# Second cross-attention of a Perceiver block: two key periods per loop step instead of one

## The chip, the cores and the metric

The kernel runs on one core of a Trainium2 chip. Five engines work side by side, each taking its instructions in the order in which they are written: TensorE (PE, matrix multiply, with its weight load PEld shown apart), VectorE (DVE), ScalarE (ACT), GpSimd (POOL) and SyncE (SP, which here only starts DMA transfers). They wait for one another by semaphores. The metric is the device time of one execution in microseconds. The kernel before took 1573.84 us, the median of three runs (1573.14 to 1574.27).

## The reference, cut to what matters

The program computes two layers of a Perceiver: each has a cross-attention to a long context, a self-attention and a mixture-of-experts network. All data is 32-bit float. The change touches only the cross-attention of the second layer. The state `x` has 128 rows (queries) of 256; the context has 12544 rows of 192.

```python
HEADS = 16
DIM_HEAD = 64
q = x @ Wq
k = context @ Wk
v = context @ Wv
...
sim = jnp.einsum('bhid,bhjd->bhij', q, k) * SCALE
attn = jax.nn.softmax(sim, axis=-1)
out = jnp.einsum('bhij,bhjd->bhid', attn, v)
...
return out @ Wo + bo
```

Here `x` is the layer-normalised state. So keys and values of 12544 rows x 1024 columns must be projected, and 16 heads of 128 x 12544 scores go through a softmax.

## The kernel before, in words

**Tiling.** Two heads make a pass (`PASSES` = 8): their 2 x 64 columns fill 128 partitions. The context is cut into 13 blocks (`NS`) of up to 1024 rows, the last with 256. A period `t` is one pass and one block, 104 in all (`NP`). What a period computes is spread over 15 turns of the loop, since the softmax needs the maximum over a whole pass before it can take exponentials. Scores of period `t` are made and kept in SBUF (a ring of 28 slots of 128 x 1024). `LAG` = 14 turns later their exponentials meet the values.

**Four kinds of matmul work in a turn.** A 32-bit matmul is issued as two matmuls in the trace.

- `scores` (L977): keys times queries, 64 rows deep. The two heads sit in rows 0 to 63 and 64 to 127 of the array and run side by side: row tiles.
- `project_keys` (L210, L213) and `project_values` (L228, L235): 192 rows deep, done as a whole part of 128 rows (`whole`, L213 and L235) and a rest of 64 rows (`tiled`, L210 and L228), where the two halves of the block run side by side as row tiles. `tiled` opens the accumulation in its PSUM bank, `whole` closes it.
- `attend` (L1069): exponentials times values, 64 columns wide. The two heads run side by side as column tiles.

**Order.** The order is written by hand (`manual_schedule`): each engine does its work as the code lists it. In one turn PE does: `attend` of period `t`-14 (column tiles), `scores` of `t`, the tiled parts of the keys of `t`+1 and of the values of `t`-12 (row tiles), then the whole parts of keys and values.

**The other engines.** ACT copies each score tile to its slot (L994), takes the exponentials (L1057) and evicts the values (L962) and half of the keys (L948). DVE keeps the running maximum (L1001), evicts the other half of the keys (L950), sums the exponentials over keys (`added`, L1096) and adds the output of `attend` to its accumulator (`attended`, L1113). POOL subtracts the maximum from the kept scores (`shifted`, L1051: the negated maximum, spread over all partitions, is added) and adds up the partial sums (L1101). SP loads the context blocks, two buffers each.

**At the end of a pass** `fold` reduces the maximum (L1024), `pass_maximum` transposes it on PE (L246) and reduces it on DVE (L1029), `pass_spread` transposes it back (L251) and ACT stores it (L1042). In the next turn but one `pass_end` sums the denominators on PE (L1124), and DVE divides (L1129, L1130). The first two periods of a pass are shifted and exponentiated at once after the maximum is known, so as to be ready for `attend`.

**PSUM.** Of eight banks, four belong to two score tiles (`ps_s`, two banks each), and four (`ps_w`) are handed round among the output of `attend`, the two halves of the keys, the two halves of the values and the small transposes. A bank can be written again once its readers are done.

Of the kernel before, what the change touches and what calls it, by code (L numbers as in the profile page):

```python
# [8 lines left out]
F32 = mybir.dt.float32  # L9
AF = mybir.ActivationFunctionType  # L10
ALU = mybir.AluOpType
# [22 lines left out]
def perceiver(ctx: ExitStack, tc: tile.TileContext, a: dict, out: bass.AP):  # L34
# [18 lines left out]
    def ps_w(name):  # L53
        return banks["pool"].tile([P, KB], F32, tag="w", name=name, bufs=banks["w"])
# [143 lines left out]
            )  # L198
        return lo, hi, h

    def project_keys(name, wk, cx, j, bank=None):

        lo, hi, h = cx
        ps = [(bank or ps_w)(f"{name}_{r}") for r in range(2)]
        js = slice(j * P, (j + 1) * P)

        def tiled():
            for r in range(2):
                rs = slice(64 * r, 64 * r + 64)
                nc.tensor.matmul(ps[r][:, :h], wk[1][rs, js], hi[rs, :h], start=True, stop=False)  # L210

        def whole(r):
            nc.tensor.matmul(ps[r][:, :h], wk[0][:, js], lo[:, r * h : (r + 1) * h], start=False, stop=True)  # L213

        return ps, tiled, whole

    def project_values(name, wv, cx, j, bank=None):

        lo, hi, h = cx
        ps = [(bank or ps_w)(f"{name}_{r}") for r in range(2)]  # L220
        js = slice(j * P, (j + 1) * P)

        def tiled():
            for kc in range(h // P):
                ks = slice(kc * P, (kc + 1) * P)
                for r in range(2):
                    rs = slice(64 * r, 64 * r + 64)
                    nc.tensor.matmul(  # L228
                        ps[r][:, ks], hi[rs, ks], wv[1][rs, js], start=(kc == 0), stop=False,
                        skip_group_check=True,  # L230
                    )

        def whole(r):
            for kc in range(h // P):
                nc.tensor.matmul(  # L235
                    ps[r][:, kc * P : (kc + 1) * P], lo[:, r * h + kc * P : r * h + (kc + 1) * P],
                    wv[0][:, js], start=False, stop=True, skip_group_check=True,
                )

        return ps, tiled, whole  # L240
# [61 lines left out]
    with tc.tile_pool(name="l0w", bufs=1) as lw:  # L302
# [8 lines left out]
        with tc.tile_pool(name="l0x", bufs=1) as work, ExitStack() as ps0:  # L311
# [195 lines left out]
            def shift(engine, t, k, banks, by):  # L507
                if banks.stop > banks.start:
                    v = ps[t][k].rearrange("p (a c n) -> p a c n", a=2, c=2)[:, banks]
                    n = banks.stop - banks.start  # L510
                    engine.tensor_tensor(v, v, by[:, banks].unsqueeze(2).to_broadcast([P, n, 2, 256]), ALU.add)  # L511
# [383 lines left out]
    with tc.tile_pool(name="l1x", bufs=1) as work:  # L895
# [31 lines left out]
        def tiles_of(s):  # L927

            n = min(SB, SK - s * SB) // P
            return [(0, 4), (4, 4)] if n == 8 else [(0, n)]  # L930
# [4 lines left out]
            place = slot if t >= NP and (t - NP) % 3 == 2 else None  # L935
            ctxs[t] = load_context(work, f"x1_ctx{t}", (t + 1) % NS, 2, place=place)

        def keys(t):
            j, s = periods[t]
            kTs[t] = work.tile([P, SB], F32, tag="kT", name=f"x1_kT{t}", bufs=2)  # L940
            cx = ctxs[t - 1]
            h = cx[2]
            pk, tiled, whole = project_keys(f"x1_k{t}", ywk, cx, j)

            def out(r):
                dst = kTs[t][:, r * h : (r + 1) * h]
                if r:
                    nc.scalar.copy(dst, pk[r][:, :h])  # L948
                else:
                    nc.vector.tensor_copy(dst, pk[r][:, :h])  # L950

            return tiled, whole, out

        def values(t):
            j, s = periods[t]
            vs[t] = work.tile([P, 8, P], F32, tag="v", name=f"x1_v{t}", bufs=3)
            cx = ctxs[t + LAG - 2]
            n = cx[2] // P
            pv, tiled, whole = project_values(f"x1_v{t}", ywv, cx, j)

            def out(r):
                nc.scalar.copy(  # L962
                    vs[t][:, r * n : (r + 1) * n, :].rearrange("p k d -> p (k d)"), pv[r][:, : n * P]
                )

            return tiled, whole, out
# [16 lines left out]
        def scores_kept(p, n):  # L983
            return p.rearrange("p (a n) -> p a n", a=2)[:, :, : n * P]

        def keep(t, sts, between=None):

            j, s = periods[t]
            ps[t] = [slot(f"x1_p{t}_{i}") for i in range(len(sts))]
            if s == 0:  # L990
                mx[j] = work.tile([P, 2, KB], F32, tag="mx", name=f"x1_mx{j}")

            def copy(i):
                nc.scalar.copy(scores_kept(ps[t][i], sts[i].shape[2] // P), sts[i])  # L994

            def maximum(i):
                n = sts[i].shape[2] // P
                if s == 0 and i == 0:
                    return
                old = scores_kept(ps[t][0], 4) if s == 0 else mx[j][:, :, : n * P]  # L1000
                nc.vector.tensor_tensor(mx[j][:, :, : n * P], sts[i], old, ALU.max)  # L1001

            if j == 0:

                for i in range(len(sts)):
                    copy(i)
                for i in range(len(sts)):
                    if s or i:
                        n = sts[i].shape[2] // P
                        m = mx[j][:, :, : n * P]  # L1010
                        old = scores_kept(ps[t][0], 4) if s == 0 else m
                        nc.vector.tensor_tensor(m, scores_kept(ps[t][i], n), old, ALU.max)
                return
            copy(0)
            if between is not None:
                between()
            if len(sts) == 2:
                maximum(1)
                copy(1)
            maximum(0)  # L1020
# [10 lines left out]
        def pass_spread(j):  # L1031
            spreads[j] = work.tile([P, 2, P], F32, tag="spread", name=f"x1_spread{j}", bufs=2)
            if j == PASSES - 1:

                final["sums"] = ps_s("x1_sums")
                final["both"] = ps_s("x1_both")
            pb = ps_w(f"x1_mb{j}")
            if j == PASSES - 1:
                final["spread"] = pb
            for u in range(2):  # L1040
                spread_column(pb[:, u * P : (u + 1) * P], negm[j][:, u : u + 1])
            nc.scalar.copy(spreads[j].rearrange("p u q -> p (u q)"), pb[:, : 2 * P])  # L1042

        def shifted(t):
            j, s = periods[t]
            for i, (p, (c0, n)) in enumerate(zip(ps[t], tiles_of(s))):
                v = p.rearrange("p (a c q) -> p a c q", a=2, q=P)[:, :, :n, :]
                engine, by = nc.gpsimd, spreads[j]
                if j == PASSES - 1 and (i == 0 or s == 0):
                    engine, by = nc.vector, final["spread"][:, : 2 * P].rearrange("p (u q) -> p u q", q=P)  # L1050
                engine.tensor_tensor(v, v, by.unsqueeze(2).to_broadcast([P, 2, n, P]), ALU.add)  # L1051

        def exponents(t):
            j, s = periods[t]
            for p, (c0, n) in zip(ps[t], tiles_of(s)):
                v = scores_kept(p, n)
                nc.scalar.activation(v, v, AF.Exp)  # L1057

        def attend(t):
            j, s = periods[t]  # L1060
            whole = j == PASSES - 1
            o = final["both"][:, 0] if whole else ps_w(f"x1_o{t}")
            total = sum(n for c0, n in tiles_of(s))
            for p, (c0, n) in zip(ps[t], tiles_of(s)):
                for c in range(n):
                    for u in range(2):
                        us = slice(64 * u, 64 * u + 64)
                        n0 = KB * u + c * P
                        nc.tensor.matmul(  # L1069
                            o[us, 0:P], vs[t][:, c0 + c, us], p[:, n0 : n0 + P],  # L1070
                            start=(c0 + c == 0 and (s == 0 or not whole)),
                            stop=(c0 + c == total - 1 and (s == NS - 1 or not whole)), skip_group_check=True,
                        )
            return o

        def added(t, i):

            j, s = periods[t]
            tiles = tiles_of(s)
            if i >= len(tiles):  # L1080
                return
            p, n = ps[t][i], tiles[i][1]
            if j == PASSES - 1:
# [13 lines left out]
            if s == 0 and i == 0:  # L1097
                sums[j] = part
                return
            total = work.tile([P, 2, P], F32, tag="sums", name=f"x1_sums{t}_{i}", bufs=2)  # L1100
            nc.gpsimd.tensor_tensor(total, sums[j], part, ALU.add)  # L1101
            sums[j] = total

# [31 lines left out]
        def projected(j0, j1):  # L1135

            for j in range(j0, j1):
                nc.tensor.matmul(
                    final["both"][:, 1, :D], oT[:, j, :], ywo[j // 4][:, j % 4, :], start=(j == 0), stop=False
                )  # L1140

        with tc.manual_schedule():
            for t in range(NP + LAG):
                before, live = t - LAG, t < NP
                e = before + 1
                end = live and periods[t][1] == NS - 1
# [249 lines left out]
```

## Time and profile before

| | us |
|---|---|
| median of three runs | 1573.84 |
| the profiled execution | 1575.52 |
| its span (first to last instruction) | 1573.8 |
| PE busy in the span | 1498.2 |
| DVE busy | 1153.5 |
| ACT busy | 997.9 |
| POOL busy | 873.4 |

The page of the profile gives one execution: busy time of each engine, the chain of work that ended last, and groups of instructions by line, with the number of instructions, busy time, the mean time of one in ns, and the idle time ahead of them with the one that ended it. The trace answers finer questions: the instructions in order of time, or the busy time of every engine in a stretch. In it matmuls overlap, so the distance between two starts tells more than the length of one. The second cross-attention fills the span from about 580 us to 1507 us, and its steady part, in which both keys and values are projected, runs from 620 us to 1437 us.

### The profile page before, as it was taken

How to read it: one execution, taken by the hardware profiler on the slowest of the kernel's cores; microseconds unless marked ns; L12 is line 12 of the kernel's file. 1: busy time of each engine (PE TensorE's matmuls, PEld its weight loads, DVE VectorE, ACT ScalarE, POOL GpSimd, SP SyncE). 2: the span in 40 equal slices, each digit the busy share in tenths (PEclk: the TensorE clock that was granted, in tenths of full speed). 3: DMA queues.
4: the chain of work that ended last, by engine and by line, in shares of the span. 5: the costliest groups of instructions: out<-in, count | busy, mean ns of one | idle time of the engine just before them, and what ended most of it. 6: DMA issues, size and time to landing. Idle time of an engine off the chain costs nothing.

```text
span 1573.8 us, 39767 instructions
## 1 busy us (share of the span) xinstructions
PE 1498.2 (95%) x17138; PEld 1151.3 (73%) x17138; DVE 1153.5 (73%) x1219; ACT 997.9 (63%) x1233; POOL 873.4 (55%) x570
## 2 busy tenths in 40 slices
PE   7999989999879999999999999999999999999979
PEld 4666656666545877787787787787787787788968
DVE  3899887999884337777777777777777777778742
ACT  4898988999883235665565565565565665666541
POOL 0488877988840000864864864864764764764400
PEclk9999999999999999999999999999999999999979
DMA  3111021211086861222222222232232232234680
GB/s 105 44 60 42 27 62 42 62 42 42 14 246 189 264 168 29 82 82 86 82 83 85 81 86 82 81 93 75 84 97 70 86 95 73 90 88 131 176 293 4
DMA packets 68737, 146.62 MB, mean 93 GB/s; under 512 B 8905, under 2 KB 27089, under 8 KB 68562
## 3 DMA queue, kind: packets, MB, share of 16 engines
q1 hardware_dynamic: 68258, 143.30, 30.7%
q8 instruction: 135, 2.21, 0.6%
q10 hardware_dynamic: 304, 0.79, 0.2%
q14 instruction: 40, 0.33, 0.1%
HBM read 143.92 MB, written 0.13 MB: 92 GB/s over the span
## 4 chain that ended last, share of the span: by engine, by line
PE 65%; DVE 7%; ACT 4%; issue 1%; DMA 1%; POOL 1%; DVEq 0%; ACTq 0%
PE x_s L977 11%; PE x_v L235 11%; PE x_k L213 10%; PE x_o L1069 10%; PE x_v L228 6%; PE x_k L210 4%; PE f_h L1302 2%; PE f_h L839 2%; PE f_py L856 2%; DVE x_part L1096 2%; PE x_both L1069 1%; ACT x_p L522 1%; PE k L213 1%; DVE x_folded L1024 1%; POOL x_p L511 1%
## 5 line engine op out<-in xcount | busy, mean ns | idle before, releaser
L1051 POOL TENSOR_TENSOR x_p<-x_p,x_spread 128x1024 f32<-128x1024 f32 (+1 forms) x186 | 427.5, 2325 | 151.4 <-ACT x_spread L1042 151.1
L511 POOL TENSOR_TENSOR x_p<-x_p,x_spread 128x512 f32<-128x512 f32 (+1 forms) x184 | 324.4, 1809 | 127.1 <-ACT x_spread L499 65.3
L1096 DVE TENSOR_REDUCE x_part<-x_p 128x256 f32<-128x1024 f32 (+1 forms) x175 | 329.6, 1923 | 0.0
L994 ACT COPY x_p<-x_s 128x1024 f32<-128x1024 f32 (+1 forms) x200 | 197.9, 996 | 179.4 <-DVE x_mx L1001 97.6
L1001 DVE TENSOR_TENSOR x_mx<-x_s,x_mx 128x1024 f32<-128x1024 f32 (+1 forms) x161 | 193.4, 1201 | 128.7 <-PE x_s L977 120.2
L1101 POOL TENSOR_TENSOR x_sums<-x_sums,x_part 128x256 f32<-128x256 f32 x161 | 117.6, 731 | 299.8 <-DVE x_part L1096 297.9
L446 ACT COPY x_p<-x_s 128x1024 f32<-128x1024 f32 x196 | 193.3, 1015 | 50.8 <-PE x_s L433 35.5
L235 PEld LDWEIGHTS x_v<-ywv_lo,x_ctx_lo 128*128 128x128 f32 x1568 | 189.3, 192 | 38.4 <-issue 36.8
L1057 ACT ACTIVATE x_p<-x_p 128x1024 f32<-128x1024 f32 (+1 forms) x200 | 197.9, 1037 | 2.2 <-DVE x_p L1051 2.0
L522 ACT ACTIVATE x_p<-x_p 128x1024 f32<-128x1024 f32 x196 | 196.5, 1063 | 0.2 <-DVE x_p L511 0.2
L235 PE MATMUL x_v<-ywv_lo,x_ctx_lo 128*128 128x128 f32 x1568 | 193.2, 276 | 0.0
L452 DVE TENSOR_TENSOR x_mx<-x_s,x_mx 128x1024 f32<-128x1024 f32 x140 | 168.1, 1220 | 32.7 <-PE x_s L433 17.8
L977 PE MATMUL x_s<-x_qT,x_kT 64*128 64x128 f32 x2744 | 177.7, 279 | 0.0
L977 PEld LDWEIGHTS x_s<-x_qT,x_kT 64*128 64x128 f32 x2744 | 160.2, 188 | 15.6 <-issue 15.4
L213 PE MATMUL x_k<-x_ctx_lo,ywk_lo 128*128 128x512 f32 (+1 forms) x364 | 171.6, 594 | 0.0
L1069 PE MATMUL x_o<-x_p,x_v 128*64 128x128 f32 x2744 | 169.6, 276 | 0.4
L962 ACT COPY x_v<-x_v 128x512 f32<-128x512 f32 (+1 forms) x208 | 116.4, 563 | 77.2 <-PE x_v L235 76.5
L1069 PEld LDWEIGHTS x_o<-x_p,x_v 128*64 128x64 f32 x2744 | 148.4, 137 | 11.0 <-issue 1.7
L228 PEld LDWEIGHTS x_v<-ywv_hi,x_ctx_hi 64*128 64x128 f32 x1568 | 105.5, 188 | 46.7 <-issue 25.4
L433 PE MATMUL x_s<-x_qz,x_kT 32*128 32x256 f32 x1568 | 118.6, 403 | 17.7 <-ACT x_p L446 16.6
L535 PE MATMUL x_o<-x_p,x_v 128*32 128x128 f32 x3136 | 113.0, 278 | 10.4 <-ACT x_p L522 7.6
L535 PEld LDWEIGHTS x_o<-x_p,x_v 128*32 128x32 f32 x3136 | 82.8, 111 | 54.5 <-ACT x_p L522 18.2
(268 smaller groups left out, 1774.0 us busy)
## 6 DMA issues: line engine op xcount, KB each, us to landing
x_ctx_lo<-in_ctxT_dram SPq DMA_DIRECT2D x119, 512.0 KB, 4.1
x_ctx_hi<-in_ctxT_dram SPq DMA_DIRECT2D x238, 128.0 KB, 4.0
f_w<-in_L_ffn_W_dram SPq DMA_DIRECT2D x32, 512.0 KB, 4.9
k_lo<-in_ctxT_dram SPq DMA_DIRECT2D x12, 512.0 KB, 8.3
f_gating<-n_kernel_gating_EDF_dram SPq DMA_DIRECT2D x8, 512.0 KB, 10.6
f_up<-L_ffn_kernel_up_EDF_dram SPq DMA_DIRECT2D x8, 512.0 KB, 10.4
f_wd<-ffn_kernel_down_EFD_dram SPq DMA_DIRECT2D x8, 512.0 KB, 10.3
k_hi<-in_ctxT_dram SPq DMA_DIRECT2D x24, 128.0 KB, 7.6
```

What stands on the lines that cost most here:

```text
L213: nc.tensor.matmul(ps[r][:, :h], wk[0][:, js], lo[:, r * h : (r + 1) * h], start=False, stop=True)
L228: nc.tensor.matmul(ps[r][:, ks], hi[rs, ks], wv[1][rs, js], start=(kc == 0), stop=False, skip_group_check=True,)
L235: nc.tensor.matmul(ps[r][:, kc * P : (kc + 1) * P], lo[:, r * h + kc * P : r * h + (kc + 1) * P], wv[0][:, js], start=False, stop=True, sk ...
L511: engine.tensor_tensor(v, v, by[:, banks].unsqueeze(2).to_broadcast([P, n, 2, 256]), ALU.add)
L522: nc.scalar.activation(ps[t][k], ps[t][k], AF.Exp)
L535: nc.tensor.matmul(os[b][32 * i : 32 * i + 32, u * P : (u + 1) * P], v[:, 2 * g + c, 17 * (2 * i + u) : 17 * (2 * i + u) + 32], p[i // 2][ ...
L977: nc.tensor.matmul(st[:, u, c * P : (c + 1) * P], kTs[t][rs, ks], qT[rs, j, :], start=True, stop=True)
L994: nc.scalar.copy(scores_kept(ps[t][i], sts[i].shape[2] // P), sts[i])
L1051: engine.tensor_tensor(v, v, by.unsqueeze(2).to_broadcast([P, 2, n, P]), ALU.add)
L1057: nc.scalar.activation(v, v, AF.Exp)
L1069: nc.tensor.matmul(o[us, 0:P], vs[t][:, c0 + c, us], p[:, n0 : n0 + P], start=(c0 + c == 0 and (s == 0 or not whole)), stop=(c0 + c == tot ...
L1096: nc.vector.tensor_reduce(part, v, AX.X, ALU.add)
```

## The change

A new function `two_periods(t)` does two turns at once, for periods 12 to 101 (`PAIRED`), in 45 steps; what comes before and after stays in the old loop. In a step PE does: `attend` of two periods, `scores` of `t` with the tiled parts of one set of projections, the whole parts of two sets of projections in a row, then the tiled parts of the second set and `scores` of `t`+1. For that the second set opens its accumulation with the whole part and closes it with the tiled part (`ahead=False`). Three kinds of step have an order of their own: those whose `t` is the last period of a pass (`ends`), the one before the last (`ends_later`), or the first (`begins`); there the maximum's transposes stand among the whole parts, one tile is shifted on DVE straight from PSUM (`beside`), and in `begins` one period's `attend` comes late, into a score bank. The sums of exponentials go through a list (`queue`), one to three tiles at a time. `keep`, `shifted` and `exponents` are split into steps by tile, and `once` makes sure that the old loop doesn't repeat what a step has done.

```diff
-    def project_keys(name, wk, cx, j, bank=None):
+    def project_keys(name, wk, cx, j, bank=None, ahead=True):
...
-                nc.tensor.matmul(ps[r][:, :h], wk[1][rs, js], hi[rs, :h], start=True, stop=False)
+                nc.tensor.matmul(ps[r][:, :h], wk[1][rs, js], hi[rs, :h], start=ahead, stop=not ahead)
...
-            nc.tensor.matmul(ps[r][:, :h], wk[0][:, js], lo[:, r * h : (r + 1) * h], start=False, stop=True)
+            nc.tensor.matmul(ps[r][:, :h], wk[0][:, js], lo[:, r * h : (r + 1) * h], start=not ahead, stop=ahead)
...
-            total = work.tile([P, 2, P], F32, tag="sums", name=f"x1_sums{t}_{i}", bufs=2)
+            total = work.tile([P, 2, P], F32, tag="sums", name=f"x1_sums{t}_{i}", bufs=3)
...
+        def two_periods(t):
+
+            at = periods[t][1]
+            ends, ends_later, begins = at == NS - 1, at == NS - 2, at == 0
+            b = [t - LAG, t + 1 - LAG]
+            nx = [u + 2 for u in b]
...
+            os_ = [(u, attend(u)) for u in b[: 1 if begins else 2] if u >= 0]
...
+            for u, o in os_:
+                taken(u, o)
+            for i in over:
+                pass_end(i)
+            context(t)
+            context(t + 1)
+            if not ends and not begins:
+                for u in nx[: 1 if ends_later else 2]:
+                    shifted(u)
...
+            sts = scores(t)
+            k, v = keys(t + 1), values(t + 1 - NS)
+            k[0]()
+            v[0]()
+            copy, maximum = keeping(t, sts)
+            copy(0)
+            if begins or ends:
+                if begins:
+                    maximum(1)
+                    copy(1)
+                else:
+                    maximum(0)
+                    fold(j)
+                for f in k[1:]:
+                    for r in range(2):
+                        f(r)
+                pass_maximum(j)
+                v[1](0)
+                pass_spread(j)
+                v[1](1)
+                for r in range(2):
+                    v[2](r)
+                first, second = (b[1], nx) if begins else (nx[0], nx[1:])
+                shift(first, 0, True)
+                shift(first, 1)
...
+            else:
+                for f in (k, v):
+                    for r in range(2):
+                        f[1](r)
...
+                maximum(1)
+                copy(1)
...
+                    maximum(0)
+                    if len(queue) > 1:
+                        summed(1)
+                    exponent(nx[0], 0)
+                    for r in range(2):
+                        k[2](r)
+                    exponent(nx[0], 1)
+                    for r in range(2):
+                        v[2](r)
+                    exponents(nx[1])
+                    summed(3, *nx)
+            k, v = keys(t + 2, False), values(t + 2 - NS, False)
+            for f in (k, v):
+                for r in range(2):
+                    f[1](r)
+            if begins:
+
+                late = attend(b[1], ps_s(f"x1_o{b[1]}")[:, 0])
+            k[0]()
+            v[0]()
...
+            for r in range(2):
+                k[2](r)
+            for r in range(2):
+                v[2](r)
+            if begins:
+                taken(b[1], late)
+            if ends:
+                summed(1, nx[1])
+            else:
+                summed(1)
+            sts = scores(t + 1)
+            copy, maximum = keeping(t + 1, sts)
+            copy(0)
...
+            if len(sts) == 2:
+                maximum(1)
+                copy(1)
+            maximum(0)
+            if ends_later:
+                fold(j)
...
+        PAIRED = range(NS - 1, NP - 2)
         with tc.manual_schedule():
             for t in range(NP + LAG):
+                if t in PAIRED:
+                    if (t - PAIRED[0]) % 2 == 0:
+                        two_periods(t)
+                    continue
```

## The prediction

> **What bounds the kernel now.** I read the shares by engine and the chain that ended last, then the second attention cut by passes, then one period in order of time.
>
> ```profile
> PE 1498.2 (95%) x17138; PEld 1151.3 (73%) x17138; DVE 1153.5 (73%) x1219; ACT 997.9 (63%) x1233; POOL 873.4 (55%) x570
> PE 65%; DVE 7%; ACT 4%; issue 1%; DMA 1%; POOL 1%; DVEq 0%; ACTq 0%
> 983.59:1100.85 117.26, 116.43 (x1289) 93.16 (x1289) 90.15 (x80) 69.83 (x90) 74.31 (x50) 1.00 0.28 84
> ```
>
> The third row is one pass (columns: stretch, length, then busy time of PE, PEld, DVE, ACT, POOL, granted clock, DMA). PE is busy in 116.4 of 117.3 us at a granted clock of 1.00. Here only fewer or denser matmuls buy time, or the waits between them. The change removes no matmul, so I look for cost between matmuls. TensorE alone, one ordinary period (start, time, line, matmuls):
>
> ```profile
> 1001.60 1.95 PE L235 MATMUL x_v<-ywv_lo,x_ctx_lo 128*128 128x128 f32 x16
> 1003.48 1.97 PE L1069 MATMUL x_o<-x_p,x_v 128*64 128x128 f32 x32
> 1005.38 2.06 PE L977 MATMUL x_s<-x_qT,x_kT 64*128 64x128 f32 x32
> 1007.26 1.03 PE L210 MATMUL x_k<-x_ctx_hi,ywk_hi 64*128 64x512 f32 x4
> 1008.13 1.06 PE L228 MATMUL x_v<-ywv_hi,x_ctx_hi 64*128 64x128 f32 x16
> 1009.11 1.98 PE L213 MATMUL x_k<-x_ctx_lo,ywk_lo 128*128 128x512 f32 x4
> 1010.93 1.95 PE L235 MATMUL x_v<-ywv_lo,x_ctx_lo 128*128 128x128 f32 x16
> 1012.81 1.97 PE L1069 MATMUL x_o<-x_p,x_v 128*64 128x128 f32 x32
> ```
>
> A period is 1012.81 - 1003.48 = 9.33 us. Single starts in this stretch give steady pitches: 0.112 for a whole x_v matmul and for a row-tiled pair, 0.109 for a column-tiled pair, 0.430 for a 512-wide one. So the six blocks need 16 x 0.112 = 1.79 (v whole), 16 x 0.109 = 1.74 (o), 1.79 (s), 0.86 (k row), 0.90 (v row), 1.72 (k whole): 8.80 us. The missing 0.53 sits where the shape changes. Whole to column: the start comes 0.093 late and the first pair takes 0.051 more, 0.144. Column to row: 0.093 and 0.101, 0.194. Row to whole: 0.097 and 0.103, 0.200. Sum 0.538.
>
> The other loss is at pass boundaries:
>
> ```profile
> 996.92 1.03 PE L210 MATMUL x_k<-x_ctx_hi,ywk_hi 64*128 64x512 f32 x4
> 997.78 0.38 PE L228 MATMUL x_v<-ywv_hi,x_ctx_hi 64*128 64x128 f32 x2
> 998.70 1.16 PE L228 MATMUL x_v<-ywv_hi,x_ctx_hi 64*128 64x128 f32 x14 [0.53 <-DVE x_oacc L1113]
> 998.35 0.29 DVE L1113 TENSOR_TENSOR x_oacc<-x_o,x_oacc 128x128 f32<-128x128 f32 x1
> ```
>
> The second bank of v is the one that o leaves, and o's eviction stands behind two x_part reductions on DVE. The period lasts 10.34 instead of 9.33.
>
> **The change part by part.** *Switches.* Two periods had six changes of shape: 2 x 0.538 = 1.076. A pair now runs column (o, o), row (s, k, v), whole (k, v, k', v'), row (k', v', s'): column to row 0.194, row to whole 0.200, and two kinds the steady stretch lacks. Whole to row: where the key projections filled an earlier stage, L213 to L210 starts 0.523 after a 0.430 pitch and the next takes 0.533, so 0.197. Row to column: at the first attention (32-row tiles to 32-column tiles) the start comes late by the same 0.09. What follows depends on the weights loaded, 64 columns wide here, so I take the 0.144 of whole to column. Its bounds are 0.09 (lateness alone) and 0.20 (the dearest switch), on 45 pairs -2.4 to +2.5 us. A pair costs 0.735 and saves 0.341, ending 18.34 us long instead of 18.67. There are 45 pairs (periods 12 to 101). 41 ordinary ones give 13.98. The three at a pass's first period put their late o between whole and row (0.144 + 0.194 for 0.197) and save 0.20 each, 0.6. The first pair has no o and saves 0.2. Sum 14.8. The spread's transposes (whole) stood between o and s and cost an extra 0.197. They now stand among whole parts: six times, 1.2. **Together 16.0 us.**
>
> *Waits removed.* Evictions of o are now ahead of the reductions, so the 1.01 us stall goes: six times, 6.1. Beside it the transposes of the pass maximum wait for a DVE copy (k ends its pitch at 972.64, they start at 973.04: 0.40), and I put 0.1 on an o bank. Six of each: 3.0. **Together 9.1**, part of which comes back below.
>
> *Does the rest keep up?* The work of the other engines for one pair, from the groups by form:
>
> ```profile
> L1051 POOL TENSOR_TENSOR x_p<-x_p,x_spread 128x1024 f32<-128x1024 f32 x165 | 386.0, 2365 | 0.2
> L1096 DVE TENSOR_REDUCE x_part<-x_p 128x256 f32<-128x1024 f32 x165 | 319.6, 1975 | 0.0
> L1001 DVE TENSOR_TENSOR x_mx<-x_s,x_mx 128x1024 f32<-128x1024 f32 x152 | 186.1, 1224 | 126.5 <-PE x_s L977 118.6
> L994 ACT COPY x_p<-x_s 128x1024 f32<-128x1024 f32 x164 | 166.0, 1012 | 158.6 <-DVE x_mx L1001 96.3 <-PE x_s L977 62.3
> L1057 ACT ACTIVATE x_p<-x_p 128x1024 f32<-128x1024 f32 x164 | 164.5, 1054 | 0.0
> L962 ACT COPY x_v<-x_v 128x512 f32<-128x512 f32 x163 | 95.8, 588 | 48.2 <-PE x_v L235 47.5
> ```
>
> DVE: 4 x 1.975 + 4 x 1.224 + 2 x 0.69 + 2 x 0.29 = 14.8 of 18.34. ACT: 4 x (1.012 + 1.054 + 0.588) + 2 x 0.584 = 11.8. POOL: 4 x 2.365 + 4 x 0.731 = 12.4. None is the bound by its sum; the order decides. I added up an ordinary pair from its first o at 0, each engine in written order, each operation 0.05 after what it waits for. PE: o to 3.49, s 3.69 to 5.48, row parts to 7.23, k whole 7.43, v whole 9.15, k' 10.94, v' 12.66 to 14.45, k' row 14.65, v' row, s' 16.41 to 18.20. The three tight places: v' starts at 12.66 and needs both v evictions from ACT, which come after the score copies, an exponent, the k copy and an exponent and end at 12.06 (**0.6 to spare**). k' at 10.94 needs the k copies, ready at 9.95. The next scores at 18.34 + 3.69 = 22.03 need the second of two DVE maxima, 20.82 (1.2 to spare). The POOL shift in front of that exponent ends at 5.43 and the exponent starts at 9.91. So an ordinary pair has no wait.
>
> This last slack is where a rule of the Trainium skill speaks against the change: "TensorEngine Tiling (Array Packing)", section PSUM Bottleneck, warns that denser tiles speed up TensorE but not eviction, which may then be the limit. Two score groups came 9.33 apart; now s' to the next s is only 3.5 us after the end of s'. By the rows, evicting one period takes the maximum of tile 1 and then of tile 0, 2 x 1.224 = 2.5 us, so it fits and costs nothing. By the rule, with all four evictions in series (2 x 1.224 + 2 x 1.012 = 4.5 us against 3.7), it costs 0.8 x 45 = 36 us and turns the sum into a loss. I take the rows, since copies and maxima already overlap in the period of before.
>
> *Pass boundaries.* Here the slack is used up. At a pass's last period: the short v leaves PE 0.17 and 0.32 early for ACT, o 0.38 for a DVE copy, s 0.51 for the second score copy, the pass maximum 0.45: 1.83 us, three times. At a first period: s 0.57, v's row part 0.37, the last scores behind the late o (it holds a score bank, and DVE reaches its eviction only after four reductions) 0.65, copies 0.2: 1.79, three times. Where the old loop takes over, 0.5. **New waits 11.4**; bounds 5 (evictions overlap better, as neighbours in the trace do by 0.04 to 0.08) and 19 (each boundary 1.3 worse).
>
> *Moved at no cost.* DMA issues are equal in number. Both context loads are now issued at the pair's head. The first buffer is free at 10.9 of the pair before, the second at 16.4; a load lands 4 us after its issue (page, last part), so by 15 and 20.5, and they are needed at 23.8 (k row) and 29.3 (k'). Without that cover PE would pay the lateness. SP carries nothing else here. In-order POOL now takes four shifts in a row, and the sums wait behind them; nothing but the pass's end reads those. The third buffer for sums and the split shift, exponent and keep functions add no instruction. Seven first shifts move from POOL (2.365) to DVE (1.213, the last pass's row), counted above.
>
> **Sum.** 16.0 + 9.1 - 11.4 = 13.7 us. The profiled execution took 1575.5 (span 1573.8); it becomes 1561.8. The median of the runs is 1573.84, so I forecast 1560.
>
> **The rivals.** *A: only switches count, and boundary waits swell* (19 instead of 11.4, or row to column at 0.20): gain 6 to 3.5, time 1568 to 1570. For it: four evictions in one queue, and only one 0.6 us slack. *B: boundaries run free* (waits 5 or less, switch at 0.09): gain 20 to 22.5, time 1551 to 1554. For it: banks are handed on in the order of release, which my additions hold only roughly. *C, slower: ACT's v eviction holds v' in every ordinary pair.* Its place is PE's wait at v' whole for x_v from ACT. ACT works through two score copies, two exponents and a k copy first. The first 0.6 us of lateness is free; then each tenth costs 4.5 us on 45 pairs. It decides from 0.6 + 13.7 / 45 = 0.9 us. At 1.2 us: 45 x 0.6 = 27 lost, 13 net, 1587. Against it: the exponent ahead has 4.5 us in hand from POOL. *D: switches don't get cheaper,* since whole to row and row to column cost double: 0.341 + 0.341 gone, pair unchanged, leaving 1572 to 1576. Against it: the L213-to-L210 starts.
>
> **How the numbers follow.** Forecast 0.58, A 0.15, B 0.15, C 0.08, D 0.04. Likeliest case alone: 1556 to 1564. Leaving out C, D and the far end of A, the 8-in-10 range is 1552 to 1568. A difference under 0.2% (3.1 us) is no more than a measurement can tell from none. Faster: forecast, A and B, 0.88; D is the same, 0.04; C slower, 0.08.
>
> **What would show it.** Right: an ordinary pair in 18.3 us of PE, four shape changes in it, no wait at v' whole, and no x_v wait for x_oacc. Boundary waits at s, x_v and x_mt of 0.2 to 0.7. Wrong: an ordinary pair of over 18.5 us, a wait of PE on ACT x_v in most pairs, or a second start after whole to row or row to column that is more than 0.25 late in all.

## The result, and the profile after

The changed kernel takes 1571.72 us, the median of 22 runs (1568.84 to 1577.58); the kernel before, in as many runs beside it, 1575.46 (1570.39 to 1580.95). The ratio is 0.9979, with a 95% interval of 0.9969 to 0.9988: some 3.3 us faster, where 13.7 were forecast. The time lies outside the stated range.

The page of the changed kernel, shares by engine and the chain that ended last:

```profile
PE 1490.1 (95%) x17138; PEld 1152.5 (73%) x17138; DVE 1156.7 (74%) x1226; ACT 987.4 (63%) x1233; POOL 858.1 (55%) x563
PE 74%; DVE 12%; ACT 7%; issue 3%; POOL 2%; DMA 1%; SPq 0%; ACTq 0%; DVEq 0%
```

PE is busy for 8 us less with the same 17138 matmuls. In the chain DVE and ACT have come up from 7% and 4% to 12% and 7%, but that says nothing about the change: on the same page 4% (DVE) and 3% (ACT) stand at L455 and L449, lines of the first attention, which the change doesn't touch. To leave such parts out, I cut both spans at the first score matmul of the second attention's first period and at that of its last one, and call what lies between them the stage. Before, then after (stretch, length, busy time of PE, PEld, DVE, ACT, POOL, granted clock, DMA share, GB/s):

```profile
0.00:579.04 579.04, 528.25 (x6505) 362.85 (x6505) 423.57 (x536) 429.83 (x495) 327.62 (x216) 0.99 0.31 92
579.04:1437.39 858.35, 849.85 (x9445) 680.18 (x9445) 655.50 (x572) 515.66 (x662) 518.07 (x340) 1.00 0.29 82
1437.39:1573.80 136.41, 120.14 (x1191) 108.31 (x1189) 74.43 (x112) 52.39 (x76) 27.76 (x14) 0.94 0.52 166
```

```profile
0.00:581.20 581.20, 532.01 (x6505) 364.92 (x6505) 423.34 (x536) 430.06 (x495) 327.60 (x216) 0.98 0.31 91
581.20:1434.63 853.43, 837.18 (x9444) 678.52 (x9445) 660.03 (x579) 504.86 (x662) 503.48 (x334) 1.00 0.29 83
1434.63:1572.00 137.37, 120.94 (x1191) 109.08 (x1189) 73.37 (x111) 52.45 (x76) 26.99 (x13) 0.93 0.51 165
```

In this pair of executions the stage itself gains 4.9 us. The same code ahead of it took 2.2 us longer, and the code behind it 1.0. The granted clock between 400 and 500 us was 0.97 before and 0.91 after, so that part varies from execution to execution. The stage is the steadier measure (two traces of one kernel, the one with four buffers below, agree in it: 844.0 us), and I use it below, with distances between the first score matmuls of two periods, which say where inside the stage the time is.

| from one period's scores to a later one's, us | before | after |
|---|---|---|
| two ordinary periods | 18.66 | 18.32 |
| six periods around a pass end that falls on the first half of a step (periods 36 to 42, 62 to 68, 88 to 94) | 51.93 each | 50.70, 50.70, 50.71 |
| six periods around the other pass ends (24 to 30, 50 to 56, 76 to 82) | 51.95, 51.94, 51.96 | 53.86, 55.52, 53.87 |

The third row loses 1.9, 3.6 and 1.9 us where the prediction's terms gave a gain.

**The ordinary step** is as it was worked out. TensorE alone, one step of the changed kernel (start, time, line, matmuls):

```profile
662.51 1.95 PE L238 MATMUL x_v<-ywv_lo,x_ctx_lo 128*128 128x128 f32 x16
664.29 1.88 PE L216 MATMUL x_k<-x_ctx_lo,ywk_lo 128*128 128x512 f32 x4
666.01 1.95 PE L238 MATMUL x_v<-ywv_lo,x_ctx_lo 128*128 128x128 f32 x16
667.89 1.13 PE L213 MATMUL x_k<-x_ctx_hi,ywk_hi 64*128 64x512 f32 x4
668.85 1.06 PE L231 MATMUL x_v<-ywv_hi,x_ctx_hi 64*128 64x128 f32 x16
669.75 1.95 PE L980 MATMUL x_s<-x_qT,x_kT 64*128 64x128 f32 x32
671.63 3.71 PE L1098 MATMUL x_o<-x_p,x_v 128*64 128x128 f32 x64
675.27 2.06 PE L980 MATMUL x_s<-x_qT,x_kT 64*128 64x128 f32 x32
```

The four whole blocks, of which the last three are shown, follow each other without a gap (664.29 to 666.01 is 1.72, the pitch of k alone). Single starts give the two new kinds of switch. Whole to row: x_k starts at 667.892 against 667.80 by the pitch, and its next pair comes after 0.533 instead of 0.430: 0.196 in all (0.197 taken). Row to column: x_o starts 0.096 late and its second pair comes after 0.160 instead of 0.109: 0.147 (0.144 taken).

**Where the rest went.** The waits of PE between 634 and 1430 us (total, times, longest). First the kernel before, all of them:

```profile
PE x_v L228 <- DVE x_oacc L1113: 3.2, 6, 0.6
PE x_mt L246 <- DVE x_kT L950: 1.4, 6, 0.3
```

Then the changed kernel, and in the last row DVE's waits on POOL in the same stretch:

```profile
PE x_s L980 <- ACT x_p L997: 9.6, 7, 2.5
PE x_s L980 <- DVE x_oacc L1140: 1.3, 3, 0.4
PE x_mt L249 <- DVE x_kT L953: 0.9, 3, 0.3
PE x_s L980 <- DVE x_mx L1004: 0.7, 3, 0.2
PE x_v L238 <- ACT x_v L965: 0.2, 1, 0.2
DVE x_part L1125 <- POOL x_sums L1130: 10.4, 3, 3.5
```

Before, DVE never waits for POOL there. Now it does three times, like the bad boundaries. One of them in order of time, on DVE, POOL, ACT and PE:

```profile
751.40 5.82 DVE L1125 TENSOR_REDUCE x_part<-x_p 128x256 f32<-128x1024 f32 x3 [1.12 <-ACT x_p L1082]
757.14 0.68 DVE L953 COPY x_kT<-x_k 128x512 f32<-128x512 f32 x1
757.74 0.28 DVE L1140 COPY x_oacc<-x_o 128x128 f32<-128x128 f32 x1
761.50 1.98 DVE L1125 TENSOR_REDUCE x_part<-x_p 128x256 f32<-128x1024 f32 x1 [3.49 <-POOL x_sums L1130]
763.40 2.54 DVE L1004 TENSOR_TENSOR x_mx<-x_s,x_mx 128x1024 f32<-128x1024 f32 x2
...
749.11 11.68 POOL L1071 TENSOR_TENSOR x_p<-x_p,x_spread 128x1024 f32<-128x1024 f32 x5 [10.69 <-ACT x_spread L1051]
760.72 0.75 POOL L1130 TENSOR_TENSOR x_sums<-x_part,x_part 128x256 f32<-128x256 f32 x1
...
764.70 1.01 ACT L997 COPY x_p<-x_s 128x1024 f32<-128x1024 f32 x1 [2.82 <-DVE x_mx L1004]
...
765.77 2.06 PE L980 MATMUL x_s<-x_qT,x_kT 64*128 64x128 f32 x32 [2.52 <-ACT x_p L997]
```

DVE makes three partial sums (`x_part`), for which there are three buffers. The fourth finds none. The first sum of a pass is not added to anything: it stays in its buffer as the accumulator until POOL adds the second to it (`x_sums<-x_part,x_part`). POOL gets there only at 760.72, after five shifts in a row, 11.7 us. DVE stands for 3.5 us, and behind the fourth sum are the two maxima of the next scores, behind the first maximum ACT's copy of a score tile, and behind that copy PE's next scores: 2.5 us.

### The profile page after: what moved, and what is told of

The parts are those of the page before. It is cut to its first block, busy times and chain, and to the rows that moved or that the text cites. A ratio compares the mean times of both kernels' runs of the same rounds, so it can differ in the third digit from the quotient of the medians.

```text
span 1572.0 us, 39688 instructions
## 1 busy us (share of the span) xinstructions
PE 1490.1 (95%) x17138; PEld 1152.5 (73%) x17138; DVE 1156.7 (74%) x1226; ACT 987.4 (63%) x1233; POOL 858.1 (55%) x563
## 4 chain that ended last, share of the span: by engine, by line
PE 74%; DVE 12%; ACT 7%; issue 3%; POOL 2%; DMA 1%; SPq 0%; ACTq 0%; DVEq 0%
PE x_v L238 12%; PE x_s L980 11%; PE x_k L216 10%; PE x_o L1098 8%; PE x_v L231 7%; PE x_k L213 6%; PE x_s L436 5%; DVE x_mx L455 4%; ACT x_p L449 3%; ACT x_p L525 2%; PE x_o L538 2%; POOL x_p L1071 2%; PE f_h L1469 2%; PE f_h L842 2%; PE f_py L859 2%
## 5 line engine op out<-in xcount | busy, mean ns | idle before, releaser
L1071 POOL TENSOR_TENSOR x_p<-x_p,x_spread 128x1024 f32<-128x1024 f32 x179 | 410.1, 2324 | 206.3 <-ACT x_spread L1051 206.3
L449 ACT COPY x_p<-x_s 128x1024 f32<-128x1024 f32 x196 | 193.5, 1016 | 51.6 <-PE x_s L436 35.8
L1082 ACT ACTIVATE x_p<-x_p 128x1024 f32<-128x1024 f32 (+1 forms) x200 | 204.7, 1048 | 17.9 <-POOL x_p L1071 13.7
L455 DVE TENSOR_TENSOR x_mx<-x_s,x_mx 128x1024 f32<-128x1024 f32 x140 | 167.9, 1221 | 33.3 <-PE x_s L436 18.7
L980 PE MATMUL x_s<-x_qT,x_kT 64*128 64x128 f32 x2744 | 175.4, 276 | 11.6 <-ACT x_p L997 9.6
L216 PE MATMUL x_k<-x_ctx_lo,ywk_lo 128*128 128x512 f32 (+1 forms) x364 | 167.3, 582 | 0.0
L1098 PE MATMUL x_o<-x_p,x_v 128*64 128x128 f32 x2744 | 161.0, 275 | 0.1
L965 ACT COPY x_v<-x_v 128x512 f32<-128x512 f32 (+1 forms) x208 | 108.3, 565 | 32.5 <-PE x_v L238 25.1
```

The lines of the kernel that those rows point to most:

```text
L449: nc.scalar.copy(ps[t][k], st[k].rearrange("p a n -> p (a n)"))
L455: nc.vector.tensor_tensor(m, st[1 - k], old, ALU.max)
L980: nc.tensor.matmul(st[:, u, c * P : (c + 1) * P], kTs[t][rs, ks], qT[rs, j, :], start=True, stop=True)
L1098: nc.tensor.matmul(o[us, 0:P], vs[t][:, c0 + c, us], p[:, n0 : n0 + P], start=(c0 + c == 0 and (s == 0 or not whole)), stop=(c0 + c == tot ...
```

## The experiments

My theory was this chain from the buffers of `x_part` to PE. The rival was that the score bank lent to the late output, and the second score copy, which stands behind two exponentials on ACT, hold the scores back in any case, and that DVE's wait is only beside it. All line numbers are those of the changed kernel.

**Four buffers.** To make room for one more, the spread maximum keeps one copy instead of two.

```diff
-            part = work.tile([P, 2, P], F32, tag="part", name=f"x1_part{t}_{i}", bufs=3)
+            part = work.tile([P, 2, P], F32, tag="part", name=f"x1_part{t}_{i}", bufs=4)
...
-            spreads[j] = work.tile([P, 2, P], F32, tag="spread", name=f"x1_spread{j}", bufs=2)
+            spreads[j] = work.tile([P, 2, P], F32, tag="spread", name=f"x1_spread{j}", bufs=1)
```

> The changed kernel with four buffers for the partial sums instead of three (room made by keeping one copy of the spread maximum instead of two). Buffer theory: DVE's fourth reduction in the step at a pass's first period no longer waits 3.5 us for POOL, so the 2.5 us wait of PE at the next step's scores goes, in each of three such steps: the six periods around one take about 51.2 us instead of 53.9, and the kernel about 1562 to 1564 against 1575 before, 8 us or more under the changed kernel. Bank theory (the late output in a score bank and the copy behind two exponents hold the scores back, whatever the buffers): the six periods stay at 53 to 54 us and the time stays near 1571.

Measured: 1560.19 us (1558.78 to 1560.62), a little under the range that I gave; ratio to before 0.9902, interval 0.9888 to 0.9917. The six periods take 51.28, 51.26 and 51.27 us. The stage is 844.0 us, 14.3 under before. DVE, POOL and PE around the same boundary:

```profile
754.70 1.97 DVE L1125 TENSOR_REDUCE x_part<-x_p 128x256 f32<-128x1024 f32 x1
756.60 2.53 DVE L1004 TENSOR_TENSOR x_mx<-x_s,x_mx 128x1024 f32<-128x1024 f32 x2
...
745.84 11.69 POOL L1071 TENSOR_TENSOR x_p<-x_p,x_spread 128x1024 f32<-128x1024 f32 x5 [10.69 <-ACT x_spread L1051]
757.47 0.75 POOL L1130 TENSOR_TENSOR x_sums<-x_part,x_part 128x256 f32<-128x256 f32 x1
...
759.92 2.06 PE L980 MATMUL x_s<-x_qT,x_kT 64*128 64x128 f32 x32
```

POOL is as late as before (its first sum comes 11.6 us after its first shift in both), but nobody waits for it. The bank and the order on ACT are the same, so the rival falls. The same kernel again, beside the last experiment:

> The first kernel once more, on the same chip as the new order: 1558 to 1562, six periods at 51.3 and 50.7 us.

It took 1560.99 us (ratio 0.9909, interval 0.9895 to 0.9924), six periods 51.27 and 50.70.

**The same buffer in the kernel before**, with nothing else changed.

```diff
-            part = work.tile([P, 2, P], F32, tag="part", name=f"x1_part{t}_{i}", bufs=3)
+            part = work.tile([P, 2, P], F32, tag="part", name=f"x1_part{t}_{i}", bufs=4)
```

> The kernel before with four buffers for the partial sums instead of three. Buffer theory: there POOL takes at most two shifts between two sums, no reduction waits for a buffer, so nothing changes: ratio 1.000 within 0.002. If it gains as well, extra buffering helps by itself and the first experiment says nothing on the change.

1575.71 us, ratio 1.000 (0.9984 to 1.0015); its two periods take 18.66 and its six 51.95, as before. (Its stage takes 860.9 us in this trace, 2.6 more, all of it within the first 14 periods, where two stretches at half the clock fall; the last section has one of them.) So the extra buffer gains nothing by itself; it helps here only where POOL's queue has been filled.

**Three buffers, POOL's order changed**: the other way to the same cause.

```diff
-                for u in second:
+                for u in second[:1]:
                     shifted(u)
                 exponents(first)
                 if begins:
                     summed(2, first)
+                    shifted(nx[1])
                     exponents(nx[0])
```

> The changed kernel with its three buffers; in the step at a pass's first period the two shifts of the last period come after the first sums on POOL instead of ahead of them. Buffer theory: the first sum is done 4.7 us sooner, DVE's fourth reduction no longer waits, but the last period's exponentials come about 1.5 us later and its output may wait about 1 us: the six periods around take 51.5 to 52.7 us instead of 53.9, the time is 1565 to 1569. Bank theory: 53 to 54 us, no gain.

1562.75 us (ratio 0.9918, interval 0.9898 to 0.9938), better than I gave it; the six periods take 51.95 to 51.97, inside what was expected. The price of the later exponentials is small:

```profile
PE x_o L1098 <- ACT x_p L1082: 1.6, 3, 0.5
```

DVE's waits on POOL's sums are gone here too. So the buffer and the order each cure it alone, and the spread's single copy in the first experiment is not what helped.

**Two buffers**: the suspected wait made longer.

```diff
-            part = work.tile([P, 2, P], F32, tag="part", name=f"x1_part{t}_{i}", bufs=3)
+            part = work.tile([P, 2, P], F32, tag="part", name=f"x1_part{t}_{i}", bufs=2)
```

> The changed kernel with two buffers for the partial sums instead of three: the suspected wait made longer. Buffer theory: at a pass's first period DVE is now held one reduction earlier, by about 2 us plus what has queued up; the six periods around it take 56.5 to 57.5 us instead of 53.9, the step at a pass's end and ordinary steps (18.32 us) stay, the time is 1579 to 1585. Bank theory: no change, 1571.

The one run took 1587.05 us, with six periods of 58.94, 59.46 and 59.71 us; ordinary steps and the other pass ends stay at 18.32 and 50.7. The direction is as expected, the size 2 us too small. DVE now stands one sum earlier, with the late output's eviction behind it, and PE waits for that eviction:

```profile
760.88 1.89 DVE L1125 TENSOR_REDUCE x_part<-x_p 128x256 f32<-128x1024 f32 x1 [6.09 <-POOL x_sums L1130]
...
763.72 2.08 PE L980 MATMUL x_s<-x_qT,x_kT 64*128 64x128 f32 x16 [6.56 <-DVE x_oacc L1140]
```

The 2 us more are time at half the granted clock after such a wait; the last section shows it.

**Two more switches in each step**, to price the change of shape on its own. On top of the first experiment:

```diff
-            k, v = keys(t + 2, False), values(t + 2 - NS, False)
+            k, v = keys(t + 2), values(t + 2 - NS)
+            k[0]()
+            v[0]()
             for f in (k, v):
                 for r in range(2):
                     f[1](r)
...
-            k[0]()
-            v[0]()
```

> As the first kernel, but the second set of projections of a step again does its row-tiled parts ahead of its whole parts: two more changes of shape in each of 45 steps (whole to row, row to whole), the same matmuls. Switch theory: an ordinary step goes from 18.32 to 18.32 + 0.197 + 0.200 = 18.72 us, the stage by 45 x 0.397 = 17.9 us. If the time between blocks comes from waits and not from the change of shape, the step stays within 0.1 us of 18.32.

An ordinary step takes 18.78 us, the first one of each pass 18.73 (18.72 expected); the stage is 860.2 us, 16.2 more than with the whole parts in a row, and the one run took 1577.85. Part of one step of this kernel:

```profile
679.54 1.98 PE L216 MATMUL x_k<-x_ctx_lo,ywk_lo 128*128 128x512 f32 x4
681.36 1.95 PE L238 MATMUL x_v<-ywv_lo,x_ctx_lo 128*128 128x128 f32 x16
683.24 1.13 PE L213 MATMUL x_k<-x_ctx_hi,ywk_hi 64*128 64x512 f32 x4
684.20 1.13 PE L231 MATMUL x_v<-ywv_hi,x_ctx_hi 64*128 64x128 f32 x16
685.25 1.98 PE L216 MATMUL x_k<-x_ctx_lo,ywk_lo 128*128 128x512 f32 x4
```

Row parts now lie between whole parts, and PE waits for nothing there. The row block from 683.24 to 685.25 takes 2.01 us against 1.86 from 667.89 to 669.75, where scores of the same shape follow. Of the 0.46 us that a step loses, 0.40 is the two switches. The rest, 0.06, is something else: in this block the second row tile of x_v starts 0.076 us behind the first, where 0.007 is usual, and the weight loads of such blocks wait for ACT's eviction of x_v (77 times, 17.3 us in all). In the first ordinary step of a pass that lag is 0.02, and the step takes the 18.73. In all the stage loses 16.2 us and not 45 x 0.46, since PE's waits for scores at pass ends, 3.9 us in all with four buffers, are gone. So the time between blocks belongs to the change of shape: two fewer switches save 0.34 in a step, two more cost 0.40.

**A better order.** With four buffers, the waits left at pass ends are those of the prediction's list. Two changes aim at them, on top of the first experiment:

```diff
-                    summed(3, *nx)
+                    summed(2 if at == NS - 3 else 3, *nx)
...
             for r in range(2):
                 k[2](r)
+            if ends_later:
+                sts = scores(t + 1)
+                copy, maximum = keeping(t + 1, sts)
+                copy(0)
             for r in range(2):
                 v[2](r)
...
-            sts = scores(t + 1)
-            copy, maximum = keeping(t + 1, sts)
-            copy(0)
+            if not ends_later:
+                sts = scores(t + 1)
+                copy, maximum = keeping(t + 1, sts)
+                copy(0)
```

> The first kernel of the study (four buffers) with two changes of order. In the step two blocks ahead of a pass's end only two sums are taken before the key eviction, not three, so that DVE's copy of the short keys comes sooner; in the step just ahead of the end ACT copies the short score tile before it evicts the values. Both aim at the waits of 0.4 to 0.6 us that the step sums still held: 0.6 us less in the six periods around each boundary, six boundaries, 3 to 4 us in all: 1556 to 1557.5. If PE's wait there ends on something else, the six periods stay at 51.3 and 50.7 us and the time at 1560.

1555.39 us (1554.2 to 1560.21), ratio to before 0.988, interval 0.986 to 0.990: the lowest of all, and a little under the range that I gave. The interval overlaps a little with that of the same kernel without the two changes (0.9895 to 0.9924), so the gain is read from the stage. The six periods around the pass ends that fall on the second half of a step go from 51.27 to 50.77 on average, the others from 50.70 to 50.43, 50.19 and 50.19; the stage is 841.2 us, 2.8 less. PE's wait for the score copies was 2.0 us in all and is now 0.5:

```profile
PE x_s L980 <- ACT x_p L997: 2.0, 4, 0.6
PE x_s L980 <- ACT x_p L997: 0.5, 1, 0.5
```

## Why the prediction was wrong

**Switches: right.** 0.341 per ordinary step was forecast, 18.66 to 18.32 is 0.34. The two kinds that I had to bound came out at 0.196 and 0.147. Read again from single starts, column to row costs 0.201, not the 0.194 of the prediction (the start is 0.100 late, not 0.093), in both kernels alike; the saving stays. Rival D (switches don't get cheaper) is out.

**Slack in the ordinary step: right.** The waits of PE show x_v on ACT once, 0.2 us, so v' never waited in an ordinary step and rival C (slower) is out. The warning of the Trainium skill in "TensorEngine Tiling (Array Packing)", PSUM Bottleneck, did not bite there: PE's waits for the score tiles lie at pass ends alone.

**Waits removed: right.** No x_v waits for x_oacc any more, and the ends in the second row of the table gain 1.2 us each. The prediction's terms for these six periods (three switch savings of 0.341, one spread transpose 0.2, removed waits 1.5, new waits 1.83) give a gain of 0.9.

**The step that failed** is in the paragraph on moves at no cost: "In-order POOL now takes four shifts in a row, and the sums wait behind them; nothing but the pass's end reads those." The sentence looks only for readers of the sums. The one who waits is the writer of what the sums read: `x_part` has three buffers, and a buffer returns when POOL has added its content. In an ordinary step the sums are taken early enough. At a pass's first period POOL has five shifts in its queue, not four, and the buffers run out. The prediction's paragraph on pass boundaries lets DVE do its four reductions there without a stop; no buffer of `x_part` is counted in it, and least of all the first partial sum of a pass, which holds its buffer until the second is added to it. The wait of 2.5 us that follows was put at nothing. The same terms as above, with 0.20 for the step with the late output and new waits of 1.79, gave a gain of 0.8 for these six periods, 51.2 us. Four buffers measure 51.27; three measure 53.86. Three times 2.6, and 1.66 for half the clock after one of the waits (below), make 9.4 us: the difference between the stage of the changed kernel, 853.4, and that with four buffers, 844.0.

**The other terms hold.** With that wait gone the stage gains 14.3 us, where the sum had 13.7. The boundary terms agree within 0.4 us for six periods (0.9 and 0.8 forecast, 1.2 and 0.7 measured); that their errors cancel so well is luck. Rival A gave a time close to the measured one, but for other reasons: the row-to-column switch is not dearer, and the boundary waits that it meant are no longer than forecast. Rival B's free boundaries need an order of their own, which the last experiment in part found.

## What to carry to other kernels

When work is put ahead of other work in an engine's queue, ask not only who reads what is delayed, but which buffers the delayed work was to give back, and who needs them next. Count such buffers through the longest queue, with the accumulator's first value as a holder of one. A loss of a few microseconds can sit in one step in thirteen and be invisible in a step that looks perfect; the distance between the same matmul in successive passes finds it.

## What the runs showed of the hardware

A wait of PE costs more than its length when the granted clock falls after it. In the changed kernel it happened after one of three waits of 2.5 us, and that boundary took 55.52 us instead of 53.86. The clock in this trace is 1.00 or 0.50, never between, and it changes only on a grid of 3.41 us. So I cut the time around the waits on this grid, the first wait in the first two rows, the second in the last two (the second number is PE's busy time in the stretch, the clock is the third number from the right):

```profile
760.85:764.26 3.41, 2.39 (x44) 2.07 (x40) 2.76 (x2) 1.03 (x1) 1.99 (x3) 1.00 0.00 0
764.26:767.67 3.41, 1.90 (x34) 1.91 (x36) 3.17 (x6) 1.65 (x2) 3.41 (x3) 1.00 0.00 0
996.37:999.78 3.41, 1.22 (x20) 1.22 (x22) 3.20 (x5) 1.01 (x1) 3.36 (x3) 1.00 0.00 0
999.78:1003.19 3.41, 3.41 (x24) 2.40 (x22) 2.48 (x4) 1.57 (x2) 3.41 (x2) 0.50 0.02 5
```

The three waits are equally long. The first is split between two stretches, and so is the third (PE busy for 2.01 and 2.28 us there); all four stay over half busy. The second falls mostly into one, in which PE is busy for 1.22 of 3.41 us, and the stretch after it runs at 0.50: half of 3.41 is the 1.7 us lost. So it matters where a wait falls on the grid, and that is different in every trace: a wait of 2.7 us near 620 us, which all nine traces have, was followed by a slow stretch in one alone, the kernel before with four buffers (PE busy 1.33 of 3.41). Where the limit lies these runs do not show: 1.41 us (with two more switches) was not followed by a slow stretch, and 1.86 us in another part of the changed kernel (231.78 to 235.19 us) was.

With two buffers the waits are 6.6 us long, and two stretches at half the clock come with each. At the second:

```profile
999.20:1002.61 3.41, 1.06 (x10) 1.09 (x12) 3.41 (x4) 0.00 (x0) 0.73 (x1) 0.50 0.00 0
1002.61:1006.02 3.41, 3.41 (x34) 3.19 (x34) 2.87 (x3) 1.01 (x1) 2.65 (x2) 0.50 0.00 0
```

PE works 4.47 us at half the clock here and so loses some 2.2 us. By the same estimate the three boundaries would take 57.2 to 57.3 us at the full clock, which lies in the range expected of two buffers.

The Trainium skill, "TensorE: Matmul & The Clock Gate", Part 1, names a free-running window of about 3.4 us, after which an idle PE is held to half the clock. The grid, the half and the long waits agree with it. That a window in which PE was still busy for 1.22 us was enough is less than the page asks for. With four buffers the waits of 2.5 us are gone, and no stretch of the stage runs at less than the full clock.
